# An order written by hand in place of a scheduler's: every engine's queue of a four-layer graph network fixed by the source, with sums one unit behind their pairs and row work spread in levels

## The chip, the cores and the metric

The kernel runs on one core of a Trainium2 chip. The metric is device time in microseconds, as a median of several executions. The core has a matrix engine (PE, with its weight loads shown apart as PEld), a vector engine (DVE), an activation engine (ACT), a general engine (POOL) and a queue engine (SP) that here issues the large loads. Each engine works through its own queue in order; an instruction that waits holds everything behind it on that engine. PSUM is the memory that PE writes its results to.

## The reference

The input is x, 4096 nodes by 64 features, and a dense adjacency matrix adj, 4096 x 4096 in float32 (67 MB) whose entries are 0 or 1. Four layers follow one another, and each reads all of adj:

```python
# each layer: x = layernorm(x + layer(x, adj))
# layer 0: mean over neighbours, linear, relu, rows scaled to length 1
h = (adj @ X + X) / (adj.sum(1) + 1);  out = relu(concat([X, h]) @ W + b);  out / |out|
# layers 1 and 3: hyperbolic attention (layer 3 with curvature 1)
adj_att = sigmoid(left[:, None] + right[None, :] + b_att) * adj   # left, right: one number a node
support = einsum('ij,ijd->id', adj_att, logmap(x[:, None], x[None, :]))
out = proj(expmap(x, support))
# layer 2: the last 100 neighbours of a row, the latest with weight 1, each earlier one half of the next
out = (mask * 0.5 ** (k - pos)) @ (x @ weight) + bias
```

`logmap` needs one number for every pair of nodes. The kernel never forms the 64-vectors of the pairs: it forms a scalar per pair, multiplies it with the attention weight, and lets PE sum over j.

## The kernel before

adj is held turned, so that a unit of work is 128 source nodes (j, one block of `BLOCKS`, 31 down to 0) against 1024 target nodes (s, one group of `GROUPS`, 3 down to 0). A layer has 4 x 32 = 128 units. `load(s, g)` (L614) brings two blocks j at once, 1 MB, on SP's queue into one of five buffers; there are 256 loads in all. The function `stream` holds the fast path that runs here; a second path, for inputs that don't fit its assumptions, is not run.

Layer 0: per load, eight matmuls (L1087) add three bfloat16 parts of x and the neighbour counts in four PSUM banks. Every second load is also looked at by DVE, whether it holds only 0 and 1 (`check`, L692; the other half of the loads is looked at in layer 2).

Layers 1 and 3 (`attend`): per unit, PE writes a score for each pair into a PSUM tile `zp` with six matmuls (L861, L864, L867, each for two halves of 512 columns), called the pairs of the unit. ACT forms the sigmoid `sig` (L869) and the square `sq` of `zp` (L873). DVE forms `t = max(zp, 0) * sig` (L875, called t1 in the text) and `t = (sq + HIGH**2) * t` (L876, t2). PE adds `xe.t` into a PSUM tile `acc` (L878), the sum of the unit. `zp` has two buffers in PSUM, `t` three.

Layer 2: the place of a neighbour from the end of its row is counted in PSUM: per unit, four matmuls (L1209, `pass_by` and `enter`) add to a tile `z` in place, ACT takes `exp` of it (L1217, `w`), and four matmuls add `w` times the features into `acc` (L1220). Two groups at a time, each with a chain of its own.

Row work is what a group of 1024 nodes needs between layers: the end of layer 0 (`end_0`), the layer norm (`norm_rows`), the tables for the attention (`prepare`), the move along the curve (`move`), the small linear maps (`linear`, L1001 to L1017), the end of layer 2 (`end_2`). These are Python generators in a list `waiting`; `tick` emits their next few steps between units of the main loop, `need` emits until a tag is through. A step can hold several operations that depend on each other. `spread_left` (L837, L842) turns the left numbers of a group into a tile that ACT can add to.

The program is emitted in this order, but the order in which each engine runs its instructions is chosen by a scheduler that lists instructions when what they depend on is done. In steady attention its PE order is: pairs of unit j+2, sum of unit j, pairs of j+3, sum of j+1. In both kernels t1 of a unit waits for the square of the same unit; both read the unit's `zp`.

Of the kernel before, what the change touches and what calls it, by code (L numbers as in the profile page):

```python
# [10 lines left out]
F32 = mybir.dt.float32  # L11
F16 = mybir.dt.float16
# [7 lines left out]
P = 128  # L20
N = 4096
D = 64
# [36 lines left out]
def gnn_stack_kernel(  # L59
# [511 lines left out]
    def stream(fits):  # L571

        with ExitStack() as st:

# [5 lines left out]
            loads = pool("f_loads", 5)  # L580
# [8 lines left out]
            waiting = []  # L589

            def tick(n):
                while n and waiting:
                    if next(waiting[0][1], False) is False:
                        waiting.pop(0)
                    else:
                        n -= 1

            def later(tag, *steps):
                def all_steps():
                    for part in steps:  # L600
                        yield from (part or ())

                waiting.append((tag, all_steps()))

            def need(tag):
                while any(t == tag for t, _ in waiting):
                    tick(1)
# [10 lines left out]
            def grp(name, bufs=None):  # L618
                kw = {"bufs": bufs} if bufs else {}
                return row.tile([P, WB, D], F32, name=name, **kw)  # L620

            def nums(name, n=WB):
                return row.tile([P, n], F32, name=name)
# [4 lines left out]
            def rsqrt(a, name):  # L628

                n = a.shape[1]  # L630
                half = row.tile([P, n], I32, name="rs_half")
                V.tensor_scalar(half, a.bitcast(I32), 1, None, ALU.logical_shift_right)
                r, t = nums(name, n), nums("rs_t", n)
                V.tensor_scalar(
                    r.bitcast(I32), half, -1.0, float(0x5F3759DF), ALU.mult, ALU.add
                )
                for _ in range(3):
                    V.tensor_mul(t, r, r)
                    V.scalar_tensor_tensor(t, t, -0.5, a, ALU.mult, ALU.mult)
                    V.scalar_tensor_tensor(r, t, 1.5, r, ALU.add, ALU.mult)  # L640
                return r
# [20 lines left out]
            ys = keep.tile([P, WB, 3 * D + 10], F16, name="ys")  # L662
            yd = keep.tile([P, WB, D + 10], F16, name="yd")
            es, ed = ys[:, :, 3 * D :], yd[:, :, D:]
            rest = (ROOT - 2.0) * UNIT
            for k in range(3):
                part = float(np.float16(rest))
                nc.gpsimd.memset(es[:, :, k], part)
                rest -= part
            nc.gpsimd.memset(ed[:, :, 0:3], 1.0)  # L670
            nc.gpsimd.memset(es[:, :, 3:5], 1.0)
            nc.gpsimd.memset(ed[:, :, 5:7], 1.0)

            def att_columns(w_att, name):


                w = row.tile([P, 2], F32, name="att_w")
# [18 lines left out]
            def curved(c, name):  # L696

                c2, sc = num(keep, name + "_c2", 1), num(keep, name + "_sc", 1)
                rsc, of_y = num(keep, name + "_rsc", 1), num(keep, name + "_of_y", 1)
                V.tensor_scalar(c2, c, -2.0, None, ALU.mult)  # L700
                V.tensor_copy(rsc, rsqrt(c, "rsc"))
                V.tensor_mul(sc, rsc, c)
                V.tensor_scalar(of_y, rsc, -((2.0 * UNIT) ** -0.5), None, ALU.mult)
                V.tensor_scalar(sc, sc, -((2.0 * UNIT) ** 0.5), None, ALU.mult)
                return c, c2, sc, rsc, of_y

            def norm_rows(x, s, v, x2_to):

                m, v2, sq = nums("n_m"), nums("n_v2"), grp("sq")
                V.tensor_reduce(m, v, AX.X, ALU.add)  # L710
                V.tensor_scalar(m, m, 1.0 / D, None, ALU.mult)
                yield 1
                V.tensor_sub(v, v, over(m))
                nc.scalar.activation(sq, v, AF.Square)
                yield 1
                yield 1
                V.tensor_reduce(v2, sq, AX.X, ALU.add)
                yield 1
                V.tensor_scalar(m, v2, 1.0 / D, 1e-5, ALU.mult, ALU.add)
                r = rsqrt(m, "n_r")  # L720
                yield 1
                V.tensor_mul(x[:, blocks(s), :], v, over(r))
                V.tensor_mul(x2_to, r, r)
                V.tensor_mul(x2_to, x2_to, v2)
                yield 1

            def prepare(s, x, att, b_att, curve, least, good):

                c, c2, sc, rsc, of_y = curve
                at, cols = blocks(s), slice(s * WW, (s + 1) * WW)  # L730
                xg, bg, rbg = x[:, at, :], b[:, at], rb[:, at]
                V.tensor_scalar(cx2[:, at], x2[:, at], c, None, ALU.mult)
                V.tensor_scalar(bg, cx2[:, at], -1.0, 1.0, ALU.mult, ALU.add)
                V.reciprocal(rbg, bg)

                V.tensor_scalar(rbg, rbg, -0.13, 0.0, ALU.max, ALU.min)

                m, y = nums("m"), grp("z0")
                V.tensor_scalar(m, rbg, sc, None, ALU.mult)
                V.tensor_mul(y, xg, over(m))  # L740
                nc.scalar.copy(ys[:, :, :D], y)
                yield 1
                nc.scalar.copy(ys[:, :, 2 * D : 3 * D], y)
                nc.scalar.copy(yd[:, :, :D], y)
                hl = row.tile([P, WB, 2], F16, name="hl")
                V.tensor_scalar(hl[:, :, 0], rbg, UNIT, None, ALU.mult)
                V.scalar_tensor_tensor(hl[:, :, 1], rbg, UNIT, hl[:, :, 0], ALU.mult, ALU.subtract)
                nc.gpsimd.tensor_copy(es[:, :, 5:7], hl)
                nc.gpsimd.tensor_copy(es[:, :, 7:9], hl)
                nc.gpsimd.tensor_copy(es[:, :, 9], hl[:, :, 0])  # L750
                nc.gpsimd.tensor_copy(ed[:, :, 3:5], hl)
                for k, of in ((7, 0), (8, 0), (9, 1)):
                    nc.gpsimd.tensor_scalar(
                        ed[:, :, k], hl[:, :, of], -2.0 / UNIT, None, ALU.mult
                    )
                V.tensor_sub(ys[:, :, D : 2 * D], y, ys[:, :, :D])
                yield 1

                g, w = nums("g"), grp("w_att")
                V.tensor_scalar(g, cx2[:, at], 1.0, 1.0 / D, ALU.add, ALU.mult)  # L760
                V.tensor_scalar(m, rbg, CUBE / UNIT, None, ALU.mult)
                V.tensor_add(w, xg, over(g))
                yield 1
                V.tensor_mul(xe[:, at, :], w, over(m))
                yield 1
                for into, rows_of in (
                    (hi_lo, ys[:, :, : 2 * D]),
                    (lo_hi, ys[:, :, D : 3 * D]),
                    (src, ys[:, :, 2 * D :]),
                    (dst, yd),  # L770
                ):
                    n = rows_of.shape[2]
                    t = aux.tile([P, WW], F16, name="aux")
                    for k in range(WB):
                        nc.tensor.transpose(  # L775
                            t[:n, k * P : (k + 1) * P], rows_of[:, k, :], ident16
                        )
                    yield 1
                    nc.scalar.copy(into[:, cols], t[:n])
                    yield 1  # L780


                q, q1, rt, t = nums("q"), nums("q1"), nums("rt"), nums("tt")
                V.tensor_scalar(q, x2[:, at], least, c, ALU.max, ALU.mult)
                V.tensor_scalar(q1, q, SMALL, None, ALU.max)
                rt = rsqrt(q1, "rt")
                yield 1
                V.tensor_mul(t, q1, rt)
                V.tensor_scalar(t, t, TOP, None, ALU.min)
                V.tensor_scalar(q1, q1, QTOP, None, ALU.min)  # L790
                nc.scalar.activation(t, t, AF.Ln, bias=1.0)
                nc.scalar.activation(q1, q1, AF.Ln, bias=1.0, scale=-1.0)
                yield 1
                f = nums("f")
                V.tensor_scalar(q, q, SMALL, SHIFT, ALU.min, ALU.add)
                V.scalar_tensor_tensor(q, q, 0.2, q, ALU.mult, ALU.mult)
                yield 1
                V.scalar_tensor_tensor(f, q1, -0.5, t, ALU.mult, ALU.add)
                V.tensor_mul(f, f, rt)
                V.scalar_tensor_tensor(f, f, SERIES0, q, ALU.add, ALU.add)  # L800
                V.tensor_scalar(m, bg, of_y, None, ALU.mult)
# [528 lines left out]
```

## Time and profile before

| | us |
|---|---|
| median of three runs (1248.55 to 1249.13) | 1248.85 |
| the profiled execution | 1248.49 |
| its span, first to last instruction | 1246.8 |
| PE busy (share of the span) | 1064.1 (85%) |
| DVE busy | 981.3 (79%) |
| ACT busy | 811.4 (65%) |
| mean DMA rate | 218 GB/s |

The time of a run is a little longer than the span of its profile. Shares of busy time are means over stages with different limits, so they are read stage by stage. The stages of the span are layer 0 (0 to 218 us), layer 1 (to 617.5), layer 2 (to 857), layer 3 (to 1213), and the tail: the last group's move and its store (to 1246.8). A line of a timeline gives start, duration, engine, source line, operation, result and operands, shape and count, and in brackets the idle time of the engine before it and what ended that. "x4" joins neighbouring instructions of one kind. A releaser is inferred from semaphores.

### The profile page before, as it was taken

How to read it: one execution, taken by the hardware profiler on the slowest of the kernel's cores; microseconds unless marked ns; L12 is line 12 of the kernel's file. 1: busy time of each engine (PE TensorE's matmuls, PEld its weight loads, DVE VectorE, ACT ScalarE, POOL GpSimd, SP SyncE). 2: the span in 40 equal slices, each digit the busy share in tenths (PEclk: the TensorE clock that was granted, in tenths of full speed). 3: DMA queues.
4: the chain of work that ended last, by engine and by line, in shares of the span. 5: the costliest groups of instructions: out<-in, count | busy, mean ns of one | idle time of the engine just before them, and what ended most of it. 6: DMA issues, size and time to landing. Idle time of an engine off the chain costs nothing.

```text
span 1246.8 us, 13844 instructions
## 1 busy us (share of the span) xinstructions
PE 1064.1 (85%) x4818; PEld 393.4 (32%) x4907; DVE 981.3 (79%) x2081; ACT 811.4 (65%) x833; POOL 49.6 (4%) x85
## 2 busy tenths in 40 slices
PE   5879788899998899798598898898889999899990
PEld 2345445232222322322232223332333333222220
DVE  5486876999997799599663347535999999999996
ACT  0021213889886787587365668767889888788870
POOL 0010101000000000000100000000000000001001
PEclk9989899899999799699699999999999999999996
DMA  7989898555554366155177887688345555565510
GB/s 280 400 338 335 313 357 324 186 175 203 202 203 169 109 201 229 68 203 186 51 268 271 295 313 265 241 295 299 134 152 201 203 202 203 182 204 204 203 34 20
DMA packets 40144, 271.83 MB, mean 218 GB/s; under 512 B 6016, under 2 KB 6272, under 8 KB 7296
## 3 DMA queue, kind: packets, MB, share of 16 engines
q1 hardware_dynamic: 37440, 269.50, 61.0%
q10 hardware_dynamic: 2624, 1.35, 0.4%
q8 instruction: 40, 0.66, 0.2%
q14 instruction: 40, 0.33, 0.1%
HBM read 269.78 MB, written 1.05 MB: 217 GB/s over the span
## 4 chain that ended last, share of the span: by engine, by line
DVE 40%; PE 40%; ACT 12%; DMA 4%; issue 3%; POOL 1%; another core or an unknown queue 0%; ACTq 0%; POOLq 0%; SPq 0%; DVEq 0%
DVE t L875 14%; DVE t L876 13%; PE acc L878 7%; PE z L1209 6%; PE acc L1220 6%; ACT w L1217 5%; PE zp L861 4%; PE zp L864 4%; PE zp L867 4%; PE acc L1087 4%; ACT sq L873 3%; DVE junk L692 3%; DMA edges<-in_adj_dram 2%; PE aux L1008 2%; PE aux L775 1%
## 5 line engine op out<-in xcount | busy, mean ns | idle before, releaser
L873 ACT ACTIVATE sq<-zp,turn 128x1024 f32<-128x1024 f32 x256 | 285.1, 1114 | 84.1 <-PE zp L867 52.9
L875 DVE SCALAR_TENSOR_TENSOR t<-zp,sig 128x1024 f32<-128x1024 f32 x256 | 311.3, 1219 | 15.3 <-ACT sq L873 12.9
L876 DVE SCALAR_TENSOR_TENSOR t<-sq,t 128x1024 f32<-128x1024 f32 x256 | 311.0, 1220 | 0.8
L869 ACT ACTIVATE sig<-left_b,right 128x1024 f32<-128x1024 f32 x256 | 292.1, 1143 | 19.9 <-DVE t L875 18.0
L878 PE MATMUL acc<-t,xe 128*64 128x512 f32 x1024 | 282.2, 624 | 16.6 <-DVE t L876 15.9
L692 DVE SCALAR_TENSOR_TENSOR junk<-edges 128x2048 bf16<-128x2048 f32 x64 | 146.4, 2288 | 94.2 <-DMA edges<-in_adj_dram 94.2
L861 PE MATMUL zp<-edges,two_i 128*128 128x512 bf16 x461 | 181.3, 393 | 37.8 <-DVE t L875 34.1
L864 PE MATMUL zp<-lo_hi,hi_lo 128*128 128x512 f16 x512 | 195.5, 382 | 3.7 <-issue 0.4
L867 PE MATMUL zp<-dst,src 74*128 74x512 f16 x512 | 196.7, 384 | 0.0
L1217 ACT ACTIVATE w<-z,at_edge 128x1024 bf16<-128x1024 f32 x128 | 136.1, 1113 | 76.3 <-PE z L1209 74.0
L861 PEld LDWEIGHTS <-two_i 128*128 128x128 bf16 x512 | 50.2, 98 | 178.9 <-issue 141.7
L1220 PE MATMUL acc<-w,halves 128*64 128x512 bf16 x512 | 80.9, 393 | 25.0 <-ACT w L1217 24.5
L1087 PE MATMUL acc<-edges,first 128*128 128x512 bf16 x240 | 79.0, 406 | 16.7 <-DMA edges<-in_adj_dram 16.3
L878 PEld LDWEIGHTS acc<-t,xe 128*64 128x64 f32 x1024 | 51.8, 136 | 124.5 <-DVE t L876 64.6
L1209 PE MATMUL z<-edges,enter 128*128 128x512 bf16 x245 | 85.4, 393 | 2.2 <-DVE k L909 1.6
L1087 PE MATMUL acc<-edges,third 128*65 128x512 bf16 x256 | 83.2, 407 | 0.8 <-issue 0.2
L867 PEld LDWEIGHTS <-src 74*128 74x128 f16 x512 | 49.4, 96 | 101.0 <-issue 42.2
L864 PEld LDWEIGHTS <-hi_lo 128*128 128x128 f16 x512 | 50.1, 98 | 86.0 <-issue 50.3
L1209 PE MATMUL z<-edges,pass_by 128*128 128x512 bf16 x237 | 75.0, 394 | 1.7 <-issue 1.5
L1220 PEld LDWEIGHTS <-halves 128*64 128x64 f16 x512 | 24.1, 108 | 75.6 <-issue 74.6
L1107 ACT COPY top<-acc 128x512 f32<-128x512 f32 x8 | 4.7, 588 | 63.7 <-PE acc L1087 63.7
L1209 PEld LDWEIGHTS <-enter 128*128 128x128 bf16 x256 | 24.2, 97 | 52.3 <-issue 28.9
(255 smaller groups left out, 784.4 us busy)
## 6 DMA issues: line engine op xcount, KB each, us to landing
edges<-in_adj_dram SPq DMA_DIRECT2D x256, 1024.0 KB, 5.0
x<-in_x_dram SPq DMA_DIRECT2D x4, 256.0 KB, 3.9
out_dram<-x ACTq DMA_DIRECT2D x4, 256.0 KB, 2.5
att_sb<-in_L_gnn_w_att_dram ACTq DMA_DIRECT2D x1, 64.0 KB, 7.3
att_sb<-in_L_gnn_att_w_dram ACTq DMA_DIRECT2D x1, 64.0 KB, 6.1
w_sb<-in_L_gnn_W_dram ACTq DMA_DIRECT2D x1, 32.0 KB, 3.7
b_sb<-in_L_gnn_b_dram ACTq DMA_DIRECT2D x1, 32.0 KB, 4.1
b_sb<-in_L_gnn_bias_dram ACTq DMA_DIRECT2D x1, 32.0 KB, 5.2
```

What stands on the lines that cost most here:

```text
L692: V.scalar_tensor_tensor(junk, a, 0.0, a, ALU.not_equal, ALU.not_equal, accum_out=odd[:, n : n + 1])
L861: nc.tensor.matmul(half, two_i, edge[:, at : at + W], start=True, stop=False)
L864: nc.tensor.matmul(half, hi_lo[:, of], lo_hi[:, to], start=False, stop=False)
L867: nc.tensor.matmul(half, src[:, of], dst[:, to], start=False, stop=True)
L869: nc.scalar.activation(sig, left_b, AF.Sigmoid, bias=right[:, j : j + 1])
L873: nc.scalar.activation(sq, zp, AF.Square, bias=turn, scale=-1.0 / UNIT)
L875: V.scalar_tensor_tensor(t, zp, 0.0, sig, ALU.max, ALU.mult)
L876: V.scalar_tensor_tensor(t, sq, HIGH**2, t, ALU.add, ALU.mult)
L878: nc.tensor.matmul(acc[h * D : (h + 1) * D, :], xe[:, j, :], t[:, h * W : (h + 1) * W], start=j == BLOCKS[0], stop=j == BLOCKS[-1],)
L1087: nc.tensor.matmul(accs[h][:m], lhs[:, j, :], edge[:, at : at + W], start=j == BLOCKS[0], stop=j == BLOCKS[-1],)
L1209: nc.tensor.matmul(z[:, h : h + W], lhs, rhs[:, h : h + W], start=j == BLOCKS[0], stop=True, skip_group_check=True,)
L1217: nc.scalar.activation(w, z, AF.Exp, bias=at_edge, scale=-LN2)
```

## The change

All engines' instructions run in the order of the source: `tc.manual_schedule()` takes the scheduler's choice away. The source is rearranged to go with it.

- Sums are kept back in a list `lag`; `flush` emits them after the pairs (or `z`) of the next unit. On PE the order is pairs of j+1, sum of j, pairs of j+2, sum of j+1, in all layers with units of that kind. In layer 2 the two groups' chains take turns, so the sum of one group's unit comes after the other's `z`.
- Row work is cut in levels: each `yield` now stands after one operation, or a few that don't depend on each other. `tick` emits one level per step: six per load in layer 0, one between t1 and t2 and two after t2 in attention, two per unit in layer 2. `both` runs two generators in turns: two halves of `prepare` (`vectors`, `ratio`), and the `end_2` of both groups.
- Row tiles of two neighbouring groups have buffers of their own (`own_rows`, `ys`, `yd`); there are six load buffers in place of five; `t` has two buffers in place of three.
- `rsqrt` is one operation shorter (no `rs_half`); `move` reads the turned sums from PSUM, without ACT's copy of them at L906; `prepare` does `src` and `dst` as separate tags; `spread_left` is a generator put in front of the waiting list; the sums of a group are copied by ACT (`sums_of`) when `flush` reaches them.
- On DVE, the small operations of both curves and of both attention columns come ahead of the first `check`, since the source has them there; the second attention column's transfer is issued behind the first's.

```diff
+            st.enter_context(tc.manual_schedule())
...
-            loads = pool("f_loads", 5)
+            loads = pool("f_loads", 6)
...
-            waiting = []
-
-            def tick(n):
+            waiting, done, lag, held = [], set(), [], []
+
+            def tick(n=1):
                 while n and waiting:
-                    if next(waiting[0][1], False) is False:
+                    if next(waiting[0], waiting) is waiting:
                         waiting.pop(0)
                     else:
                         n -= 1
...
+            def both(*steps):
+                steps = list(steps)
+                while steps:
+                    steps = [part for part in steps if next(part, waiting) is not waiting]
+                    yield
...
+            def flush():
+
+                while lag:
+                    lag.pop(0)()
+
+            def sums_of(s, acc):
+                to = row.tile([P, W], F32, name="sums%d" % (s % 2))
+                nc.scalar.copy(to, acc[0])
+                return to
...
-            def rsqrt(a, name):
-
-                n = a.shape[1]
-                half = row.tile([P, n], I32, name="rs_half")
-                V.tensor_scalar(half, a.bitcast(I32), 1, None, ALU.logical_shift_right)
-                r, t = nums(name, n), nums("rs_t", n)
+            def rsqrt(a, r, t):
+
                 V.tensor_scalar(
-                    r.bitcast(I32), half, -1.0, float(0x5F3759DF), ALU.mult, ALU.add
+                    r.bitcast(I32), a.bitcast(I32), -0.5, float(0x5F3759DF), ALU.mult, ALU.add
                 )
+                yield
                 for _ in range(3):
                     V.tensor_mul(t, r, r)
+                    yield
                     V.scalar_tensor_tensor(t, t, -0.5, a, ALU.mult, ALU.mult)
+                    yield
                     V.scalar_tensor_tensor(r, t, 1.5, r, ALU.add, ALU.mult)
-                return r
+                    yield
...
+                            flush()
+                            sig = sb.tile([P, WW], F32, name="sig")
+                            nc.scalar.activation(
+                                sig, left_b, AF.Sigmoid, bias=right[:, j : j + 1]
+                            )
+                            sq = sb.tile([P, WW], F32, name="sq")
+                            nc.scalar.activation(sq, zp, AF.Square, bias=turn, scale=-1.0 / UNIT)
+                            t = sb.tile([P, WW], F32, name="t")
+                            V.scalar_tensor_tensor(t, zp, 0.0, sig, ALU.max, ALU.mult)
+                            tick()
+                            V.scalar_tensor_tensor(t, sq, HIGH**2, t, ALU.add, ALU.mult)
+                            tick(2)
+
+                            def add(acc=acc, j=j, t=t):
+                                if not acc:
+                                    acc.append(ps.tile([P, W], F32, name="acc"))
+                                for h in range(2):
+                                    nc.tensor.matmul(
+                                        acc[0][h * D : (h + 1) * D, :], xe[:, j, :],
+                                        t[:, h * W : (h + 1) * W],
+                                        start=j == BLOCKS[0], stop=j == BLOCKS[-1],
+                                    )
+
+                            lag.append(add)
+                    lag.append(
+                        lambda s=s, acc=acc: later(
+                            move(layer, s, x, x_new, sums_of(s, acc), curve), behind(s, x_new)
+                        )
                     )
...
+                            behind[i] = here
+                            flush()
+
+                            w = sb.tile([P, WW], BF16, name="w2", bufs=3)
+                            nc.scalar.activation(w, z, AF.Exp, bias=at_edge, scale=-LN2)
...
+                            lag.append(add)
+                            tick(2)
+                lag.append(
+                    lambda two=two, accs=accs: later(
+                        both(*[end_2(s, sums_of(s, acc)) for s, acc in zip(two, accs)])
+                    )
+                )
```

In the changed kernel the lines named here stand at: pairs L1256, L1259, L1262; sigmoid L1267; square L1271; t1 L1273; t2 L1275; sum L1282; layer 2's z L1369 and sum L1385; `check` L721.

## The prediction

> **What bounds the kernel now.** I read the busy times by stage first, then the instructions of one stretch inside each loop, in order of time, then the waits of the group's costliest lines. The stages (layers 0 to 3, then the tail) are, with columns window, us, busy time of PE, PE's weight loads, DVE, ACT, POOL, granted clock, DMA share, GB/s:
>
> ```profile
> 0.00:218.00 218.00, 169.78 (x916) 94.79 (x934) 147.06 (x423) 36.99 (x61) 14.90 (x33) 0.93 0.89 335
> 218.00:617.50 399.50, 351.88 (x1403) 118.95 (x1427) 354.42 (x616) 304.99 (x304) 10.31 (x14) 0.93 0.50 171
> 617.50:857.00 239.50, 211.31 (x1118) 72.79 (x1141) 110.72 (x292) 161.50 (x167) 7.27 (x17) 0.98 0.78 274
> 857.00:1213.00 356.00, 326.96 (x1367) 105.82 (x1389) 344.87 (x633) 304.85 (x299) 12.76 (x19) 1.00 0.53 181
> 1213.00:1246.80 33.80, 4.16 (x17) 1.09 (x17) 24.19 (x119) 3.12 (x5) 4.39 (x3) 0.65 0.05 19
> ```
>
> Layer 0 is held by its loads (0.89 of the DMA engines). Layer 3 is held by DVE (345 of 356 us) and layer 1 by the same loop plus stretches where DVE idles (354 of 399.5). These two attention layers are 60% of the span. A stretch of layer 3:
>
> ```profile
> 990.08 1.08 PE L878 MATMUL acc<-t,xe 128*64 128x512 f32 x4
> 990.23 1.11 ACT L873 ACTIVATE sq<-zp,turn 128x1024 f32<-128x1024 f32 x1 [0.29 <-PE zp L867]
> 991.08 1.23 DVE L876 SCALAR_TENSOR_TENSOR t<-sq,t 128x1024 f32<-128x1024 f32 x1
> 991.10 0.39 PE L861 MATMUL zp<-edges,two_i 128*128 128x512 bf16 x1
> 992.21 0.38 PE L867 MATMUL zp<-dst,src 74*128 74x512 f16 x1
> 992.30 1.22 DVE L875 SCALAR_TENSOR_TENSOR t<-zp,sig 128x1024 f32<-128x1024 f32 x1
> 992.51 1.08 PE L878 MATMUL acc<-t,xe 128*64 128x512 f32 x4
> 992.67 1.11 ACT L873 ACTIVATE sq<-zp,turn 128x1024 f32<-128x1024 f32 x1 [0.29 <-PE zp L867]
> 993.55 1.23 DVE L876 SCALAR_TENSOR_TENSOR t<-sq,t 128x1024 f32<-128x1024 f32 x1
> 993.57 0.39 PE L861 MATMUL zp<-edges,two_i 128*128 128x512 bf16 x1
> ```
>
> The reader is to see the period, 991.08 to 993.55 = 2.47 us per unit (one 128 x 1024 block of pairs), and that DVE goes from L875 to L876 to L875 with no idle; PE and ACT are ready before it. This works because PE's order lets pairs run ahead: the pairs that start at 991.10 are squared at 992.67 and used by the L875 that starts after 993.55, a unit later than the L875 at 992.30 beside them. Units overlap by two.
>
> ```profile
> 419.48 1.11 ACT L873 ACTIVATE sq<-zp,turn 128x1024 f32<-128x1024 f32 x1 [2.21 <-PE zp L867]
> 420.62 1.23 DVE L875 SCALAR_TENSOR_TENSOR t<-zp,sig 128x1024 f32<-128x1024 f32 x1 [2.10 <-ACT sq L873]
> ```
>
> This is the other regime, at a place where the run-ahead is lost: L875 (t1 below) starts only when the square of its own unit has ended (420.59, then 0.03), although it reads zp and sig, not sq. DVE idles 2.10 us for it.
>
> ```profile
> 400.09 0.63 PE L1001 MATMUL aux<-ident,x 128*64 128x128 f32 x4 [3.91 <-DVE x L992]
> 413.39 0.58 PE L861 MATMUL zp<-edges,two_i 128*128 128x512 bf16 x1 [3.46 <-DVE t L875]
> ```
>
> Here row work stands in PE's queue ahead of the next group: about 20 us with one or two units, at 390-413, 499-513 and 600-617. That is what layer 1 has over layer 3.
>
> **The change part by part.** The profiled execution took 1248.49 us against a median of 1248.85, and its span is 1246.8; I forecast the span and add the 1.7 us around it.
>
> *Attention loop, both layers (the big term).* The source order of the changed kernel, which now is the engines' order, is: pairs of unit j+1, sum of unit j, pairs of j+2, sum of j+1. The sum runs one unit behind, not two. The pairs of j+2 stand in PE's queue behind the sum of j, which waits for t2 of j (L876 before, L1275 after). t1 of j+2 still waits for the square of j+2 (its wait is on a count of ACT's finished instructions that includes the square). So there is a closed chain over two units, from the rows above: t2 1.22; to the sum 0.06 (392.19 to 392.24 and 385.80 to 385.86 elsewhere in the timeline); sum to next pairs 1.02 (990.08 to 991.10); pairs 1.11 to the last one's start and 0.38 for it, 1.49; to the square 0.08 (992.59 to 992.67); square 1.11; to t1 0.04; t1 to t2 1.25. Sum 6.27 us per two units, 3.14 per unit. The other engines need less per unit: DVE 2.47 with small operations (2.67 with the change's mean of row operations), PE 1.02 + 1.49 = 2.5, ACT 1.14 + 1.11 = 2.25. So the chain binds: 128 units x 3.135 = 401 us per layer, against 128 x 2.47 = 316. DVE is then late for nothing but this chain; its row work hides in the 0.5 us left, except what stands between t1 and t2, where the changed order puts 108 small operations in layer 1 and 124 in layer 3. Half of these lie on the turn that matters, at 0.11 us (0.08 + 0.03) each: 6 us per layer.
>
> *Layer 1.* 401 + 6 + 5 for the first fill (pairs, square, t1, t2 without overlap). Three things join the chain at single places: PE row matmuls (two L1001 of 1.06 and two L1008 of 1.97, 6.1 per group; 24 in four groups, of which half falls in PE's idle time: 12); at each group's end ACT's copy of the sums now stands ahead of the next group's sigmoid and waits for the last sum, about 3 each: 12; and row Squares and tanh on ACT, which wait for a DVE operation queued behind a t2 (1.22 + 0.69 + 0.4 = 2.3 each): 10. They fall on each other's waits in part; I take half of 34, 17, with ends 0 and 34. The boundary stretches of 20 us vanish, since the row work comes in levels. Sum 429, range 407 to 447 (399.5 before).
>
> *Layer 3.* 401 + 6 + 3 + half of (8 PE transposes, 9 for three boundaries, 12 ACT waits) = 424, range 405 to 438 (356 before).
>
> *Layer 2.* Two chains take turns; the changed order puts z of one group between the other's z and its sum. Before:
>
> ```profile
> 700.48 2.12 ACT L1217 ACTIVATE w<-z,at_edge 128x1024 bf16<-128x1024 f32 x2 [1.43 <-PE z L1209]
> 701.64 0.62 PE L1220 MATMUL acc<-w,halves 128*64 128x512 bf16 x4 [0.36 <-ACT w L1217]
> 702.20 0.62 PE L1209 MATMUL z<-edges,pass_by 128*128 128x512 bf16 x2
> 704.03 2.12 ACT L1217 ACTIVATE w<-z,at_edge 128x1024 bf16<-128x1024 f32 x2 [1.43 <-PE z L1209]
> ```
>
> A turn of two units takes 3.55 us (700.48 to 704.03). PE's part of it is eight z matmuls, 1.92, and two sums of 0.555, 1.11: 3.03; the rest it waits for the exponentials. After, an exponential (1.11) with its two hops (0.3 together) takes 1.41 and PE has 0.96 + 0.555 = 1.515 of other work meanwhile, so PE is bound: 128 x 1.515 = 194, with row matmuls on PE (13, as in the layer before), fill 3, and 8 for stalls of ACT's queue behind row work (bounds 0 and 30): 218, range 200 to 245 (239.5 before).
>
> *Layer 0.* A sixth load buffer and row work at six levels a load. A group takes about 50.8 us, against 42 at the 400 GB/s that 31-62 us reached; of the 35 us in four groups I take 11. Against it all of both curves' and att columns' small chained operations stand before the first adjacency check on DVE, which ran at 20.8 before and now waits for the second att transfer, about 33 (the third check waited to 35 in the profile): 6 lost, since five or six buffers stand full. 213, range 192 to 230 (218 before). The loads' queue (SP) is moved past nothing else.
>
> *Tail.* Each of three inverse roots loses one operation of 0.2, and the copies at L906 (two of about 0.6, one hidden) go; other operations keep their order: 33.8 - 0.6 - 0.6 - about 1.5 for reordering = 31, range 28 to 34. Double row tiles and the third t buffer taken away cost nothing of themselves: t of j+2 needs the sum of j to be read, which the chain contains anyway.
>
> Sum: 213 + 429 + 218 + 424 + 31 = 1315, and 1.7: **1317 us**. The break-even is at 2.9 us per unit: 1246.8 - 213 - 218 - 31 - 51 of layer extras = 734, over 256.
>
> **A rule against a row.** With the chain, PE idles about 0.6 us per unit. In layer 2 before, PE has gaps of 0.36 to 0.44 in each turn and the granted clock there (700-712) is 1.00; where gaps of 3.4 to 4.3 us stand (500-530) it is 0.66 and the pair matmuls take 0.63 for 0.38. By the rows the clock stays, and the sum is as above. The Trainium skill's page "TensorE: Matmul & The Clock Gate" says in "A second HAM failure mode: psum-queue depth-cycling" that short idles between groups of matmuls that cycle PSUM banks can make the clock swing between half and full. By that rule, as an estimate with the clock low half of the time, the sum would lie midway between the forecast and rival 3 below, near 1465; rival 3 itself is priced from the rows alone. I follow the row: its gaps are nearest in size.
>
> **Rivals.** (1) *Faster: the chain is not closed*, because t1 need not wait for its square. Then 1.22 + 0.06 + 2.51 + 0.08 + 1.25 (pairs to t2, t1 beside the square) = 5.1 per two units, 2.56, under DVE's 2.67, and the layers take 342 + 22 and 342 + 17: 213 + 364 + 218 + 359 + 31 + 1.7 = 1187. It decides if the unit falls under 2.9. Against it: the row at 420.62, and 12.9 us of idle time put down to the square on L875. (2) *Slower still: stalls of a fixed order add up.* Nothing can slip past a waiting instruction: ACT's row copies and Squares hold the next exponential or sigmoid, PE's transposes hold pairs. All terms at their upper ends: 230 + 447 + 245 + 438 + 34 + 1.7 = 1396; two thirds of the way 1370. For it: the 0.5 us of slack per unit is less than one big row operation (0.69). (3) *PE's clock falls in the attention loops*: pairs by the row spacing at 413-415 (0.43 each, 0.63 the last: 2.8), the sum doubled to 2.0: 8.6 per two units, 4.3, +297: 1614. Against it the 1.00 in layer 2. (4) *The order doesn't change at all*: excluded, since sums stand one unit behind and not two.
>
> **How the numbers follow.** The forecast has 0.70 (own range 1270 to 1350: unit 3.05 to 3.2, and the stages' ends half used); rival 1 with cases between it and 2.9 per unit 0.13; rival 2 0.14; rival 3 0.02; within 0.2% 0.01 (a no-change bound of about 2.5 us, what this kernel's runs can tell). The range leaves out rival 1's lower part and rival 3 and the top of rival 2: 1250 to 1380. Faster 0.13, same 0.01, slower 0.86.
>
> **What would show it.** Right: in attention a period of 6.3 us per two units; t1 idle before it with the square as releaser in nearly every unit; pair matmuls idle behind sums that wait for t2; DVE about 78% busy in layers 1 and 3, no 20 us boundary stretches; layer 2 with PE over 90% busy. Wrong: a unit at 2.5 to 2.7 with DVE full (rival 1), ACT or PE idle behind row instructions for many units (rival 2), pair matmuls at 0.6 us (rival 3).

## The result

The changed kernel takes 1405.95 us (median of four runs, 1404.91 to 1406.76) against 1248.99 for the kernel before: a ratio of 1.1256, 95% interval 1.1237 to 1.1276. The direction and the place were as predicted; the size was not. The forecast of 1317 lies 89 us too low, and 1406 is outside the range of 1250 to 1380.

The stages of the profile after, with the same columns as before (window, us, busy time of PE, PE's weight loads, DVE, ACT, POOL, granted clock, DMA share, GB/s). The boundaries are the first pairs of layer 1, the first work of layer 2, the first pairs of layer 3, and the end of the last t2:

```profile
0.00:225.20 225.20, 169.28 (x928) 94.22 (x929) 149.16 (x413) 36.90 (x60) 15.42 (x39) 0.92 0.86 333
225.20:692.50 467.30, 354.80 (x1426) 108.65 (x1424) 356.75 (x593) 295.96 (x298) 10.02 (x14) 0.95 0.40 144
692.50:912.50 220.00, 212.05 (x1133) 66.58 (x1133) 112.72 (x290) 160.11 (x160) 8.39 (x17) 0.98 0.81 293
912.50:1377.60 465.10, 346.26 (x1414) 102.69 (x1412) 362.85 (x644) 298.86 (x299) 12.43 (x20) 0.96 0.38 139
1377.60:1404.00 26.40, 2.79 (x11) 1.13 (x11) 17.19 (x98) 1.43 (x3) 2.83 (x2) 0.54 0.04 14
```

In the table the bound between layer 3 and the tail isn't the same on both sides: before, it lies at the end of the last pairs, here at the end of the last t2. Set at the end of the last pairs here too (1373.9 us), layer 3 is 461.4 and the tail 30.1.

| stage | before | forecast | after |
|---|---|---|---|
| layer 0 | 218 | 213 | 225.2 |
| layer 1 | 399.5 | 429 | 467.3 |
| layer 2 | 239.5 | 218 | 220.0 |
| layer 3 | 356 | 424 | 465.1 |
| tail | 33.8 | 31 | 26.4 |

DVE is as busy in layer 1 as it was (357 us, 354 before), but over 467 us. A steady stretch of layer 1, from its timeline:

```profile
603.00 1.22 DVE L1275 SCALAR_TENSOR_TENSOR t<-sq,t 128x1024 f32<-128x1024 f32 x1
604.28 1.08 PE L1282 MATMUL acc<-t,xe 128*64 128x512 f32 x4 [0.21 <-DVE t L1275]
605.29 0.40 PE L1256 MATMUL z<-edges,two_i 128*128 128x512 bf16 x1
606.40 0.38 PE L1262 MATMUL z<-dst,src 74*128 74x512 f16 x1
606.87 1.11 ACT L1271 ACTIVATE sq<-z,turn 128x1024 f32<-128x1024 f32 x1 [0.57 <-ACT sig L1267]
608.02 1.23 DVE L1273 SCALAR_TENSOR_TENSOR t<-z,sig 128x1024 f32<-128x1024 f32 x1
609.28 1.23 DVE L1275 SCALAR_TENSOR_TENSOR t<-sq,t 128x1024 f32<-128x1024 f32 x1
```

These seven lines are the forecast chain, each starting where the one above lets it: t2, sum, pairs, square, t1, t2. It closes in 609.28 - 603.00 = 6.28 us for two units; the forecast was 6.27. The groups of the page say what each end of the chain waits for over both layers:

```profile
L1273 DVE SCALAR_TENSOR_TENSOR t<-z,sig 128x1024 f32<-128x1024 f32 x256 | 313.1, 1223 | 216.5 <-ACT sq L1271 216.1
L1282 PE MATMUL acc<-t,xe 128*64 128x512 f32 x1024 | 289.3, 644 | 216.3 <-DVE t L1275 215.8
```

Before, the same two groups idled 15.3 and 16.6 us:

```profile
L875 DVE SCALAR_TENSOR_TENSOR t<-zp,sig 128x1024 f32<-128x1024 f32 x256 | 311.3, 1219 | 15.3 <-ACT sq L873 12.9
L878 PE MATMUL acc<-t,xe 128*64 128x512 f32 x1024 | 282.2, 624 | 16.6 <-DVE t L876 15.9
```

So the loop is as forecast, and what the forecast missed lies around it. The starts of successive t2 give the time of each unit. If every unit is counted at 3.14, layer 1 has 61 us over and layer 3 57, of which 57 and 54 lie in intervals above 4 us (22 in layer 1, 24 in layer 3). This is one of them, at a group's end:

```profile
1265.33 1.23 DVE L1275 SCALAR_TENSOR_TENSOR t<-sq,t 128x1024 f32<-128x1024 f32 x1
1266.61 1.08 PE L1282 MATMUL acc<-t,xe 128*64 128x512 f32 x4
1267.73 0.58 ACT L624 COPY sums<-acc 128x512 f32<-128x512 f32 x1 [3.70 <-PE acc L1282]
1268.22 1.15 ACT L1267 ACTIVATE sig<-left_b,right 128x1024 f32<-128x1024 f32 x1
1269.27 1.10 ACT L1271 ACTIVATE sq<-z,turn 128x1024 f32<-128x1024 f32 x1
1270.40 1.23 DVE L1273 SCALAR_TENSOR_TENSOR t<-z,sig 128x1024 f32<-128x1024 f32 x1 [3.85 <-ACT sq L1271]
```

ACT stands 3.70 us at the copy of the sums, which waits for the last sum. The next sigmoid and square are ready to run behind it (the square's pairs ended at about 1266.7), but stay behind it. Both units then in flight are late by 3.2 us. With a row operation on ACT that waits for a DVE operation queued behind a t2 (the Square at L955, a store issued from ACT's queue at L1405) it is the same, 2.6 to 2.7 us each.

Not every stall is ACT's. In layer 1's linear maps PE's own row matmuls stand ahead of the next pairs and wait for DVE:

```profile
434.71 1.03 PE L1064 MATMUL aux<-ident,x 128*64 128x128 f32 x4 [2.89 <-DVE x L1055]
435.54 0.63 PE L1256 MATMUL z<-edges,two_i 128*128 128x512 bf16 x1
437.67 0.63 PE L1262 MATMUL z<-dst,src 74*128 74x512 f16 x1
438.39 1.11 ACT L1271 ACTIVATE sq<-z,turn 128x1024 f32<-128x1024 f32 x1 [6.23 <-issue]
439.40 0.56 ACT L1069 COPY x_t<-aux 64x512 f32<-64x512 f32 x1
434.00:440.80 6.80, 6.09 (x16) 1.98 (x17) 1.79 (x3) 2.41 (x3) 0.00 (x0) 0.50 0.00 0
```

The interval, from t2 at 432.74 to t2 at 440.80, is 8.1 us long. The pairs start late, and they run slowly besides: a pair matmul takes 0.63 us in place of 0.39, and the granted clock from 434.0 to 440.8 us is 0.50 (last line, columns as in the stages). ACT's copy comes only after the late square. The slow clock can make an interval above 4 us without any row operation, as 50 us before the end, between t2 at 1355.92 and t2 at 1361.18:

```profile
1354.81 1.22 PE L1282 MATMUL acc<-t,xe 128*64 128x512 f32 x4 [3.18 <-DVE t L1275]
1355.95 0.61 PE L1256 MATMUL z<-edges,two_i 128*128 128x512 bf16 x1
1358.06 0.64 PE L1262 MATMUL z<-dst,src 74*128 74x512 f16 x1
1358.78 1.11 ACT L1271 ACTIVATE sq<-z,turn 128x1024 f32<-128x1024 f32 x1 [3.47 <-PE z L1262]
1355.60:1359.00 3.40, 3.40 (x10) 1.02 (x10) 1.51 (x2) 0.22 (x1) 0.00 (x0) 0.50 0.00 0
```

In layer 1 64 of 768 pair matmuls take over 0.5 us, in layer 3 44 of 768.

### The profile page after: what moved, and what is told of

It is laid out like the page before. It is cut to its first block, busy times and chain, and to the rows that moved or that the text cites. A ratio compares the mean times of both kernels' runs of the same rounds, so it can differ in the third digit from the quotient of the medians.

```text
span 1404.0 us, 13864 instructions
## 1 busy us (share of the span) xinstructions
PE 1085.2 (77%) x4907; PEld 373.3 (27%) x4907; DVE 998.7 (71%) x2037; ACT 793.3 (56%) x819; POOL 49.1 (3%) x91
## 5 line engine op out<-in xcount | busy, mean ns | idle before, releaser
L1273 DVE SCALAR_TENSOR_TENSOR t<-z,sig 128x1024 f32<-128x1024 f32 x256 | 313.1, 1223 | 216.5 <-ACT sq L1271 216.1
L1282 PE MATMUL acc<-t,xe 128*64 128x512 f32 x1024 | 289.3, 644 | 216.3 <-DVE t L1275 215.8
L1271 ACT ACTIVATE sq<-z,turn 128x1024 f32<-128x1024 f32 x256 | 284.0, 1110 | 223.2 <-issue 97.7
L1275 DVE SCALAR_TENSOR_TENSOR t<-sq,t 128x1024 f32<-128x1024 f32 x256 | 313.3, 1224 | 3.1
L1267 ACT ACTIVATE sig<-left_b,right 128x1024 f32<-128x1024 f32 x256 | 291.9, 1140 | 15.5 <-DVE x L1055 11.6
L1256 PE MATMUL z<-edges,two_i 128*128 128x512 bf16 x512 | 210.8, 412 | 0.0
L1262 PE MATMUL z<-dst,src 74*128 74x512 f16 x512 | 202.7, 396 | 0.0
L1259 PE MATMUL z<-lo_hi,hi_lo 128*128 128x512 f16 x512 | 202.0, 395 | 0.0
L721 DVE SCALAR_TENSOR_TENSOR junk<-edges 128x2048 bf16<-128x2048 f32 x64 | 146.4, 2287 | 64.8 <-DMA edges<-in_adj_dram 64.3
L1282 PEld LDWEIGHTS acc<-t,xe 128*64 128x64 f32 x1024 | 52.2, 139 | 346.7 <-DVE t L1275 334.2
L1256 PEld LDWEIGHTS <-two_i 128*128 128x128 bf16 x512 | 51.1, 100 | 214.9 <-issue 186.4
L1385 PE MATMUL acc<-w,halves 128*64 128x512 bf16 x512 | 80.6, 395 | 2.9 <-ACT w L1378 2.7
L1369 PE MATMUL z<-edges,enter 128*128 128x512 bf16 x256 | 79.2, 391 | 2.6 <-DVE enter L1321 2.6
L1369 PE MATMUL z<-edges,pass_by 128*128 128x512 bf16 x248 | 78.4, 397 | 0.0
L1262 PEld LDWEIGHTS <-src 74*128 74x128 f16 x512 | 51.0, 100 | 72.8 <-issue 11.0
L1259 PEld LDWEIGHTS <-hi_lo 128*128 128x128 f16 x512 | 52.0, 102 | 34.8 <-issue 5.8
L1194 PEld LDWEIGHTS <-first 128*128 128x128 bf16 x256 | 24.5, 101 | 54.5 <-DVE first L1117 16.9
L1194 PEld LDWEIGHTS <-third 128*65 128x65 bf16 x256 | 29.5, 115 | 35.1 <-issue 6.2
L770 PE MATMUL aux<-ident,ys 128*128 128x128 f16 (+1 forms) x192 | 17.2, 255 | 25.0 <-DVE ys L827 24.9
```

The lines of the kernel that those rows point to most:

```text
L721: V.scalar_tensor_tensor(junk, a, 0.0, a, ALU.not_equal, ALU.not_equal, accum_out=odd[:, n : n + 1])
L1194: nc.tensor.matmul(accs[h][:m], lhs[:, j, :], edge[:, at : at + W], start=j == BLOCKS[0], stop=j == BLOCKS[-1],)
L1256: nc.tensor.matmul(half, two_i, edge[:, at : at + W], start=True, stop=False)
L1259: nc.tensor.matmul(half, hi_lo[:, of], lo_hi[:, to], start=False, stop=False)
L1262: nc.tensor.matmul(half, src[:, of], dst[:, to], start=False, stop=True)
L1267: nc.scalar.activation(sig, left_b, AF.Sigmoid, bias=right[:, j : j + 1])
```

## The experiments

Two theories were to be told apart. The first: the loop is the closed chain through the sum, the pairs and the square, and the rest of the gap is made by ACT's row operations that wait in its queue. The second: the row operations themselves, one by one between the units on DVE and PE, are what takes the time. A third question was whether the fixed order or the rearranged source costs. All experiments are edits of the changed kernel unless it is said otherwise.

**Sums two units behind.**

```diff
-            def flush():
-                while lag:
+            def flush(keep=0):
+                while len(lag) > keep:
...
-                            flush()
+                            flush(1)
...
-                            t = sb.tile([P, WW], F32, name="t")
+                            t = sb.tile([P, WW], F32, name="t", bufs=3)
...
-                            w = sb.tile([P, WW], BF16, name="w2", bufs=3)
+                            w = sb.tile([P, WW], BF16, name="w2", bufs=2)
```

> The changed kernel with sums two units behind the pairs in attention (three t buffers, two w2 buffers to make room). Closed-chain theory: the chain t2, sum, pairs, square, t1, t2 then spans three units, 6.28/3 = 2.1 us, so DVE binds again at 2.5 to 2.7 us per unit in place of 3.14; 256 units give back 110 to 160 us: 1250 to 1295. Rival (the extra time is row operations on DVE and PE between the units): it stays within 20 us of 1406.

Measured: 1290.79 us (ratio to before 1.0357, 1.0332 to 1.0381), 115 us less than the changed kernel. The median time from one t2 to the next falls from 3.33 to 2.70 in both layers. The third buffer of t does not explain it: with two, t1's idle time ended with the square (216.1 of 216.5 us), not with the sum that sets a t free. From the page:

```profile
L1273 DVE SCALAR_TENSOR_TENSOR t<-z,sig 128x1024 f32<-128x1024 f32 x256 | 311.8, 1218 | 109.2 <-ACT sq L1271 109.1
L1282 PE MATMUL acc<-t,xe 128*64 128x512 f32 x1024 | 285.7, 637 | 8.6 <-DVE t L1275 8.5
```

The sum's wait for t2 has gone from PE (216 to 9 us), and half of t1's wait for the square. Most of the rest (65 of 109 us) stands in intervals above 4 us, the stalls at single places: those at the Square (5.9 us) and at the linear maps (about 8) stay as long as they were, those at the copies of the sums no longer appear.

**Sums not behind at all.**

```diff
-                            lag.append(add)
+                            add()
```

> The changed kernel with the sum of a unit straight after its own t2, ahead of the next unit's pairs. Closed-chain theory: one unit then takes the whole 6.28 us, so 256 x 3.14 = 804 us more: about 2200. Rival (t1 and the square, or DVE's own work, set the loop): under 100 us more.

Measured: 2586.65 us (one run), well over the 2200 that the theory gave. One unit of layer 1's timeline, from t2 to t2:

```profile
602.07 1.22 DVE L1275 SCALAR_TENSOR_TENSOR t<-sq,t 128x1024 f32<-128x1024 f32 x1
603.35 1.98 PE L1282 MATMUL acc<-t,xe 128*64 128x512 f32 x4 [3.77 <-DVE t L1275]
605.25 0.61 PE L1256 MATMUL z<-edges,two_i 128*128 128x512 bf16 x1
607.96 1.11 ACT L1271 ACTIVATE sq<-z,turn 128x1024 f32<-128x1024 f32 x1 [6.15 <-issue]
609.11 1.23 DVE L1273 SCALAR_TENSOR_TENSOR t<-z,sig 128x1024 f32<-128x1024 f32 x1 [5.46 <-ACT sq L1271]
610.37 1.23 DVE L1275 SCALAR_TENSOR_TENSOR t<-sq,t 128x1024 f32<-128x1024 f32 x1
```

The chain is closed over one unit, but it takes 8.30 us and not 6.28. PE now idles 3.77 us in each unit, and its matmuls run slow: 1.98 for the sum (1.08 in the changed kernel) and 0.61 for a pair matmul (0.40). The granted clock in 600 to 660 us is 0.61; in the changed kernel, with idle stretches of 0.2 and 1.1 us ahead of the sums, it is 0.99 there. (1.90 + 2.71 from sum to pairs to square, against 1.01 + 1.58, makes 2.0 of difference: the whole of it.) So the time follows the chain for lags of none and one, once the slower clock is counted; with a lag of two the chain is shorter than DVE's own work and no longer shows. A slow PE clock, which rival 3 had priced for a lag of one, is what a lag of none brings.

**t1 without the pair scores.**

```diff
-                            V.scalar_tensor_tensor(t, zp, 0.0, sig, ALU.max, ALU.mult)
+                            V.scalar_tensor_tensor(t, left_b, 0.0, sig, ALU.max, ALU.mult)
```

> The changed kernel, but t1 reads the left numbers in place of the pair scores (the max of the scores is left out, so what it computes is not the layer). t1 then has no reason to wait for the square; t2 still has. Closed-chain theory: the chain loses one t1, 1.25 us, and is 5.0 us per two units, 2.5 each, so DVE's 2.5 to 2.7 binds: 100 to 140 us less than the changed kernel with the stalls of row work left, 1270 to 1305. Rival (t1's wait for the square is not on the path): within 20 us of 1406.

Measured: 1299.37 us (1.0394, 1.036 to 1.0429), 107 us less, with a median unit of 2.81. t1's wait for the square is a link of the chain; taking out this one link opens it nearly as far as the second unit of lag did (2.81 and 2.70), with the lag left at one.

**ACT's row operations later.** Two to three levels stand between an operation and ACT's use of it, and a group's sums are copied one unit later; the store, the Squares, tanh and copies are treated alike.

```diff
                 nc.gpsimd.tensor_mul(w, xg, u)
+                yield
+                yield
+                yield
                 nc.scalar.activation(sq, u, AF.Square)
...
-                    lag.append(
-                        lambda s=s, acc=acc: later(
+                    lag.append((1,
+                        lambda s=s, acc=acc: later(
```

> The changed kernel with its lag of one, but every row operation on ACT put two or three levels later than the operation that it waits for, and the copy of a group's sums one unit later. Theory (an ACT row operation that waits holds the next square and empties the pipeline, 2.5 to 3.3 us each): the stalls at copies of sums, row squares, stores and tables go, 40 to 60 us in both layers together: 1345 to 1366. Rival (the stalls are made by DVE's or PE's row work itself): within 12 us of 1406.

Measured: 1363.67 us (1.0936, 1.0917 to 1.0956), 42 us less. The excess in intervals above 4 us falls from 57 and 54 to 25 and 26 us. From the first matmul of a layer's units to that of the next layer, layer 1 falls by 30 us, and layer 3, to its last pairs, by 24, while layer 2 grows by 14: one interval between exponentials, at 744 us, is 9.7 us long. That it is later row work of layer 1 which runs into layer 2 is likely, but no run shows it. So about half of the excess was ACT's queue, with what follows from its stalls (pair matmuls over 0.5 us fall from 64 and 44 to 25 and 29). The other half stands at the row operations' places still. In layer 1's linear maps it is PE's row matmuls, as the lines above show (one such interval is still 7.8 us long); for the rest PE's and DVE's parts were not separated.

**The startup.** The operations of the attention columns and curves are emitted after the tenth and twelfth load of layer 0.

```diff
-                att1, att3 = att_columns(w_att1, "att1"), att_columns(w_att3, "att3")
-                curve1, curve3 = curved(c1, True, "k1"), curved(c3, False, "k3")
+                att_load(w_att1, "att1")
+                att_load(w_att3, "att3")
...
+                        if s == GROUPS[0] and g == 6:
+                            att1, att3 = att_columns("att1"), att_columns("att3")
+                        if s == GROUPS[0] and g == 4:
+                            curve1, curve3 = curved(c1, True, "k1"), curved(c3, False, "k3")
```

> The changed kernel, with the operations of both attention columns and both curves emitted after ten and twelve loads instead of ahead of the first check (the transfers are issued where they were). Theory: the first check no longer waits to 41.0 us, load buffers come free earlier, and layer 0 gives back 8 to 12 us: 1394 to 1398. Rival (layer 0 is held by its later loads and row work in any case): within 3 us of 1406.

Measured: 1399.44 us (1.1195, 1.1164 to 1.1226), 6.5 us less, a little short of the 8 to 12 expected. The first check of the changed kernel, from the view of its line (least, median and greatest ns, then the first and last start in us), and in this run, from its timeline:

```profile
L721 DVE SCALAR_TENSOR_TENSOR junk<-edges x64: 2277/2286/2293, 41.0 to 898.1; 128x2048 bf16<-128x2048 f32 x64
```

```profile
25.84 2.29 DVE L727 SCALAR_TENSOR_TENSOR junk<-edges 128x2048 bf16<-128x2048 f32 x1
```

The first check comes 15 us earlier, and layer 1's first pairs start at 217.4 in place of 225.3. Before, they started at 216.6: of the 8.7 us that layer 0 had lost, this one stretch was 7.9.

**The scheduler's order for the changed source.**

```diff
-            st.enter_context(tc.manual_schedule())
```

> The changed source without the fixed order: the scheduler chooses again. If the fixed order is what costs, the pairs run two ahead again and the time is 1220 to 1290. If the rearranged source (levels, buffers, two chains in turns) costs of itself, it stays over 1350.

Measured: 1197.29 us (0.96, 0.9584 to 0.9616): 209 us less than the changed kernel, 4% faster than the kernel before, and below the 1220 to 1290 expected. The stages of the four layers and the line of t1:

```profile
0.00:218.00 218.00, 166.81 (x910) 92.95 (x925) 143.84 (x421) 36.33 (x59) 9.29 (x40) 0.91 0.88 340
218.00:573.00 355.00, 331.95 (x1377) 108.70 (x1402) 341.15 (x590) 300.40 (x295) 11.09 (x12) 0.99 0.53 191
573.00:806.00 233.00, 217.35 (x1149) 71.90 (x1171) 116.78 (x297) 170.66 (x173) 11.03 (x17) 0.98 0.78 281
806.00:1165.80 359.80, 331.12 (x1379) 106.77 (x1403) 347.51 (x645) 300.69 (x295) 13.91 (x20) 0.98 0.49 178
```

```profile
L1272 DVE SCALAR_TENSOR_TENSOR t<-z,sig 128x1024 f32<-128x1024 f32 x256 | 312.0, 1220 | 15.3 <-ACT sq L1270 7.2
```

The rearranged source costs nothing; the fixed order, with its sums one unit behind, costs all of it. Under the scheduler DVE's wait at t1 is 15.3 us as before, and layer 1 takes 355 us in place of 399.5: the three standstills of 20 us have gone. Layer 2's gain is partly there too (233, from 239.5), so that part is not the fixed order's.

**What of the source makes that gain.** Two runs. In the kernel before, layer 1's row work at two steps a unit for all groups:

```diff
-                1, x1, x_2, curve1, (2, 1, 1, 1), lambda s, x: linear(s, x, w2_sb, supports)
+                1, x1, x_2, curve1, (2, 2, 2, 2), lambda s, x: linear(s, x, w2_sb, supports)
```

> The kernel before, with one number changed: layer 1 emits two steps of row work per unit for all groups, not for the first alone. Theory on the gain that the changed source has under the scheduler (1197 against 1249): layer 1's row work no longer runs into the next group's start, where 20 us stood still three times. If late row work makes those stretches, they go here too: 1190 to 1215. Rival (they come from large steps whose operations depend on each other, however early): within 10 us of 1249.

Measured: 1246.31 us (0.9973, 0.9949 to 0.9997); layer 1 is 400 us still. Emitting the coarse steps earlier doesn't help. And in the changed source under the scheduler, the next group's left tile only at the group's end:

```diff
-                        if g < 6 and next_left is None and n + 1 < NW and not held:
+                        if g < 0 and next_left is None and n + 1 < NW and not held:
```

> The changed source under the scheduler, but the next group's left tile is asked for only at the group's end, as before. If the early left tile is what frees the boundaries: 1215 to 1240. If it is the levels: within 8 us of 1197.

Measured: 1209.99 us (0.968, 0.9647 to 0.9713), 13 us of the 52. The early left tile is a quarter of the gain; the time lies between what the two theories gave. The remainder is in the levels, the buffers and the rest of the rearrangement, which were not separated.

**The order mended, and the same source scheduled.** Sums two behind, ACT's gaps and the late startup together; then that source without the fixed order.

```diff
-                            flush()
+                            flush(keep=1)
... (with the gaps and the startup of the runs above)
```

> The fixed order mended: sums two units behind, ACT's row operations and the copies of sums later as in the run with gaps, and the startup as in the run before this. If the three causes add: 1291 - 42 - 10 = 1239, from 1215 to 1250, about equal to the kernel before. If the gaps do nothing once units overlap by two: 1280.

> The same source as the mended order, with the scheduler's order in place of the fixed one. If only the order of the engines' queues matters and the scheduler repairs it from any source, 1185 to 1200, as the changed source under the scheduler; if the gaps and the startup help it too, 1175 to 1187.

Measured: 1247.67 us (0.9975, 0.9963 to 0.9988) with the fixed order and 1195.57 (0.9556, 0.9534 to 0.9578) with the scheduler's. The three causes add up to within 6 us (1291 - 42 - 6.5 = 1242), and the mended order is level with the kernel before. The scheduler still does 52 us better on the same source. From first to last pairs, 23 of these are in layer 1 (376.4 against 353.0) and 22 in layer 3 (379.4 against 357.3), and 7 pass between layer 1's last pairs and layer 2's first z. t1 waits for the square for 67.4 us in the mended order, and for 32.2 under the scheduler. The mended source gains at most little over the plain changed source under the scheduler (1195.6 and 1197.3, measured beside different runs of the kernel before; the ratios are 0.9556 and 0.9600).

## Why the prediction was right and wrong

- **The loop** was right to 0.01 us in two units, with its place and its mechanism. Only the sign named for it was off in one point: t1 idles for the square in every second unit of the steady stretch (0.80 us before t1 at 605.30, none at 608.02), not in nearly every one. The lags of none and two, and t1 without the scores, each move the time the way the chain says; the lag of none adds a slower clock to it.
- **"They fall on each other's waits in part; I take half of 34, 17"** is the step that failed, with its twin in layer 3. The stalls of row work hardly overlap: they come one after another at different units. With the 6 us for small operations, the forecast had 23 and 20 us over the loop; the profile has 61 and 57. Taken whole, the listed terms would have been 40 and 35, so the list was short too. The copy of the sums was priced rightly (3 each, measured 3.2), and the Square at 2.3 was measured at 2.7. The linear maps' row matmuls were priced at their own length, 6.1 a group, half of it hidden; what they cost is the wait for DVE that holds the pairs behind them (three intervals with 14 us of excess, and 11 more in the later steps of these maps). Left out were the stores from ACT's queue in layer 3 (8 us) and, but for 8 us of transposes in layer 3, the work on the attention's tables: at the start of the layers, where these are made, the intervals above 4 us have 14 us of excess in layer 1 (to 308 us) and 22 in layer 3 (to 1001 us).
- **The clock behind a stall** was put at nothing, though the prediction's own row (0.66 where gaps of 3.4 to 4.3 us stand) had it. Six slow pair matmuls hold the square back by 1.1 us (2.71 against 1.58 from the pairs to the square, in the run with no lag). At this price the 64 and 44 pair matmuls over 0.5 us are about 12 us in layer 1 and 8 in layer 3, an estimate that takes all of them to be on the chain; they lie in part in the intervals named above.
- **Layer 0** was wrong in sign. The first check came at 41.0 us, not at 33 (and before, the third check ran at 36.2, not at 35): behind the second transfer (33.9) there were still 7 us of operations of 0.2 us that depend on each other. And the 11 us of better transfers came to less: from 45 us on, the loads move 355 GB/s, against 342 before. The startup run shows that 8 us of the 12 missed are the late check.
- **Layer 2** was right to 2 us. PE is busy for 212 of 220 us. The run under the scheduler shows that turns of two chains give part of this without the fixed order.
- **The tail**, bounded as before, took 30.1 us, within a microsecond of the forecast; the 26.4 of the table starts later.
- **The clock in the loop** stayed, as the row from layer 2 had it: 0.99 from 600 to 660 us, where PE's idle stretches were up to 1.4 us until 656, and pair matmuls at 0.40. Over the whole of layers 1 and 3 it was 0.95 and 0.96, with the stalls in it. The swing that the Trainium skill describes in "TensorE: Matmul & The Clock Gate" ("A second HAM failure mode: psum-queue depth-cycling") for short idles was not seen in it.
- **Rival 2** was the case that came true in size, and it was given 0.14. Its own ends (447 and 438 for the layers) were too low as well, since they were built from the same list.

## What to carry to other kernels

When a program's order is fixed by hand, count how many units each loop-carried chain spans (here: vector result, sum, next pairs, activation, vector) and divide its length by that number. If this exceeds the bounding engine's own need, one more unit of lag is worth more than any trimming of operations. Then look at every engine that serves the loop, here ACT and PE, for an operation that waits for something young: in this fixed order each cost nearly its whole wait (2.6 to 3.2 us on ACT), and the waits added. Try the rearranged source under the scheduler before the order is fixed, since the two changes can have opposite signs.

## What the runs showed of the hardware

With an idle stretch of 3.77 us in every 8.3 us, PE's granted clock was 0.61 and its matmuls took 1.6 to 1.8 times as long; with idle stretches of 0.2 and 1.1 us in turns, one in each unit of 3.14 us, it was 0.99. So the loop's penalty for too little overlap is more than linear: the chain of 6.28 us became 8.30 when PE waited longer. In the changed kernel a clock of 0.50 also followed single idle stretches of 2.89 us (before 434.7) and 3.18 us (before 1354.8), though one of 3.19 us (before 1251.6) left it at full speed. The Trainium skill's page "TensorE: Matmul & The Clock Gate" states in "What's actually happening" that the half clock comes after at least one idle window of about 3.4 us. The 3.77 and the 1.1 us lie on the two sides of that figure; the 2.89 and 3.18 lie under it, so here somewhat shorter waits could be enough.
